# Attention of a gated cross-attention and MoE layer: probabilities transposed in 32x32 blocks on VectorE, V multiplied in eight PE tiles of 32 rows, both layernorms applied by ScalarE

## The chip, the cores and the metric

The kernel runs on one core of one Trainium2 chip. The metric is device time in microseconds (us), the median of the runs of one kernel. Everything is fp32.

## The reference, cut to what matters

Two residual steps on x (4 x 1024 x 256). The first is cross-attention with 16 heads of 64 on a context of 64 rows per batch, with the queries multiplied onto the result; the second is a mixture of 8 experts, two per token.

```python
n = _layernorm(x)
qh = einsum('bld,hdk->hblk', n, w_qs)          # kh, vh: the same from the context, 64 rows per batch
attn = softmax(einsum('hblk,hbmk->hblm', qh, kh))
out = einsum('hblm,hbmk->hblk', attn, vh) * qh
x = x + tanh(g_xattn) * (out.reshape(heads together) @ w_proj.T + b_proj)
n = _layernorm(x)
x = x + tanh(g_ffn) * sum over the 2 chosen experts e of weight_e * (silu(n @ w1[e]) @ w2[e])
```

## The kernel before, in words

**Tiling.** The 4096 tokens are cut into 8 groups of 512 (`NG`), two per batch (`GB`), and each group into 4 tiles of 128 tokens (`T`). The 16 heads are handled as 8 pairs (`NP`), since two heads of 64 fill 128 partitions. Queries are held transposed: `qT` is two blocks (`halves`, L359), each of 4 pairs x 512 tokens, with the 2 x 64 head columns on the partitions.

**Attention of a group.** `queries` (L366) makes one pair's `qT` in one PSUM bank and ScalarE copies it out. `probabilities` (L381) takes one tile of 128 tokens: 8 matmuls of 128 columns give the scores `sc` of all 16 heads, VectorE takes the maximum and subtracts it, ScalarE takes Exp, VectorE sums and inverts, GpSimd multiplies (L404). The result `pr` has the tokens on the partitions. `transpose_probabilities` (L408) turns it round on TensorE: 8 transposes of 128x128 into two PSUM banks, and two copies by ScalarE into `aT` (L415), one per bank. `attend` (L419) takes two pairs of two heads: 4 matmuls, each of 64 rows (the keys of one head) by 64 columns (its V) over all 512 tokens, in four different quarters of the PE array, into two banks `po`; VectorE then multiplies each bank onto the queries in place (L437). `project` (L439) multiplies with `wp` and adds into x.

**Layernorm.** `ln_stats` (L250) makes mean and variance on VectorE, the root on ScalarE and the reciprocal on VectorE. `ln_norm` (L266) has VectorE make `xn` (subtract the mean, multiply by 1/std, L277), TensorE transposes it and ScalarE copies it to `nT`. It runs once per group ahead of the attention ("a") and once after it ("b"); there `keep_b` also goes to DRAM for the experts' gathers.

**V.** `values` (L333) makes V of two batches in four PSUM fills, and ScalarE copies each in four pieces into one SBUF block `vs`, with the keys of even heads on the lower 64 partitions and those of odd heads on the upper 64.

**Order of the work.** The main loop (L1109 to L1164) goes through the groups g and, inside, the tiles t. In step (g, t) it writes down, in this order, the probabilities of tile t, the transposes of the tile before, pieces of the coming queries (`parts`, L1099), at t = 1 the four `attend` calls of group g-1 with queries between them, at t = 2 and 3 the projection of group g-1, the second layernorm of group g-2, the routing, and from g = 6 on pieces of the experts' work (`pieces`). The framework plans each engine's order from this text order and from when operands and buffers are due by its own plan, so neighbouring steps can be interleaved; `keep_in_program_order` and `issue_after` pin single instructions. After the attention the rest of the experts' slots (28 in all) run one after the other.

**Buffers.** PSUM has 8 banks: `ps1` has four single ones, which `pq`, `pa`, `po`, `pp`, `pt` and others share, and `ps2` has two of two banks, which the scores use. SBUF blocks of 8 KB per partition come in three shares (L93): "group" (8), "hidden" (2) and "weight" (7). "weight" holds `wq`, `wp`, two blocks of keys and `vs`, and from g = 6 on the experts' weights as blocks come free. Those weights, the lists of tokens and all first loads are issued on SP's queue, in order.

Of the kernel before, what the change touches and what calls it, by code (L numbers as in the profile page):

```python
# [8 lines left out]
F32 = mybir.dt.float32  # L9
# [12 lines left out]
def kernel(  # L22
# [15 lines left out]
):  # L38

# [83 lines left out]
    normed = dram.tile([N, D], F32, tag="normed", name="normed")  # L123
    lists = dram.tile([E * N + BEHIND, 2], I32, tag="lists", name="lists")
# [66 lines left out]
    vs = block([P, B, NP, DK], "vs", "weight")  # L191
# [58 lines left out]
    def ln_stats(groups, name):  # L250
        n = len(groups) * T
        mv = small.tile([P, n, 2], F32, tag="mv", name=f"mv_{name}")
        for i in range(n):
            st = small.tile([P, 6], F32, tag="st", name=f"st_{name}_{i}")
            first = nc.vector.bn_stats(st, xg[groups[i // T]][:, i % T, :])
            if i == 0 and name[0] == "a":
                tc.keep_in_program_order(first)
            nc.vector.bn_aggr(mv[:, i, :], st)
        rstd = small.tile([P, n, 1], F32, tag="rstd", name=f"rstd_{name}")
        root = nc.scalar.activation(rstd, mv[:, :, 1:2], AF.Sqrt, bias=eps)  # L260
        if name in ("a0", "a1"):
            tc.keep_in_program_order(root)
        nc.vector.reciprocal(rstd, rstd)
        return {g: (mv[:, k * T : (k + 1) * T], rstd[:, k * T : (k + 1) * T]) for k, g in enumerate(groups)}

    def ln_norm(g, stats, name):  # L266
# [8 lines left out]
        for t in range(T):  # L275
            xn = keep[:, t, :] if keep else work.tile([P, D], F32, tag="xn", name=f"xn_{name}_{g}_{t}")
            nc.vector.tensor_scalar(  # L277
                xn, xg[g][:, t, :], mv[:, t, 0:1], rstd[:, t, :], ALU.subtract, ALU.mult
            )
            for c in range(NC):  # L280
                nc.tensor.transpose(  # L281
                    pt[c][:, t * P : (t + 1) * P], xn[:, c * P : (c + 1) * P], ident
                )
# [49 lines left out]
    def values(ctxT):  # L333

        n = 512 // P
        for b0 in range(0, B, 2):
            for p0 in range(0, NP, n):
# [9 lines left out]
                pvv = pv.rearrange("p (q j r k) -> p q j r k", j=2, r=2, k=DK)  # L347
                q0 = p0 // 2
                for i in range(2):
                    to = vs[:, b0 + i].rearrange("p (q r) k -> p q r k", r=2)  # L350
                    for j in range(2):
                        nc.scalar.copy(
                            to[j * M : (j + 1) * M, q0 : q0 + n // 2],
                            pvv[i * M : (i + 1) * M, :, j],
                        )
                yield


    def halves(name, share="group"):  # L359

        return [block([P, NP // 2, G], f"{name}_{i}", share) for i in range(2)]

# [18 lines left out]
    def probabilities(g, t, qT):  # L381

        sc = ps2.tile([P, NP // 2, 2, 2, M], F32, tag="ps2", name=f"sc_{g}_{t}")
        for p in range(NP):
            nc.tensor.matmul(  # L385
                sc[:, p // 2, :, p % 2, :],
# [5 lines left out]
        scv = sc.rearrange("p q r j m -> p (q r j) m")  # L392
# [15 lines left out]
    def transpose_probabilities(g, t, pr, aT):  # L408
        prv = pr.rearrange("p (i j) m -> p i (j m)", j=2)
        n = 512 // P  # L410
        for p0 in range(0, NP, n):
            pt = bank(f"pa_{g}_{t}_{p0}")
            for i in range(n):
                nc.tensor.transpose(pt[:, i * P : (i + 1) * P], prv[:, p0 + i, :], ident)  # L414
            nc.scalar.copy(  # L415
                aT[p0 // n][:, :, t * P : (t + 1) * P], pt.rearrange("p (i q) -> p i q", i=n)
            )

    def attend(g, q, qT, aT):  # L419

        po = [bank(f"po_{g}_{2 * q + j}") for j in range(2)]
        for r in range(2):
            for j in range(2):
                half = slice(j * M, (j + 1) * M)
                i = q * 2 + r
                nc.tensor.matmul(  # L428
                    po[j][r * DK : (r + 1) * DK],
                    vs[half, g // GB, i, :],  # L430
                    of_pair(aT, i)[half],
                    start=True,
                    stop=True,
                )
        for j in range(2):
            own = of_pair(qT, 2 * q + j)
            nc.vector.tensor_tensor(own, po[j], own, ALU.mult)  # L437
# [671 lines left out]
    for g in range(NG + 3):  # L1109
        attention_ends = g >= NG  # L1110
        if g < NG:
            qT, aT = qTs[g], halves(f"aT_{g}", "hidden" if g % 2 and g + 1 < NG else "group")
            held[g] = (qT, aT)
# [5 lines left out]
        for t in range(T):  # L1119
            if g < NG:  # L1120
                pr = probabilities(g, t, qT)
# [5 lines left out]
            if 0 < g <= NG and t == 1:  # L1127
                for q in range(NP // 2):
                    attend(g - 1, q, *held[g - 1])
                    for h, p in products[q : q + 1]:  # L1130
                        queries(h, qTs[h], [p])
                products = products[NP // 2 :]
# [5 lines left out]
            if g == 0:  # L1138
                for _ in range(value_parts[t]):
                    next(pending_values)  # L1140
            if 0 <= before_last < NG and t < 2:
# [73 lines left out]
```

## Time and profile before

| | |
|---|---|
| time, median of 3 runs | 889.93 us (888.75 to 890.03) |
| the profiled execution's own time | 918.12 us |
| its span, first to last instruction | 916.3 us |
| mean granted TensorE clock in it | 0.986 |
| busy: PE, PEld, DVE, ACT, POOL | 871.4, 657.5, 327.8, 263.9, 403.0 us |

PE is TensorE's matmuls, PEld its weight loads, which lie beside matmuls; DVE is VectorE, ACT ScalarE, POOL GpSimd, SP the queue of most DMAs. A line of a group reads: line, engine, operation, output <- inputs, shapes, count | busy us, mean ns of one | idle time of the engine ahead of it, and what ended it. Busy time is the union of the records, and a matmul's record is longer than the time until the next can start, so "mean ns" of matmuls is a latency and not a rate. Each fp32 matmul of the program appears as two passes, each with a weight load of its own: `pq` is 128 matmuls in the program and x256 in the trace. Transposes appear once.

The profiled execution is 28 us longer than the median of the runs. It holds two odd stretches: ScalarE idles from 403.8 to 421.2 us and TensorE waits for it, and from 490 to 512 us TensorE is busy for 12.8 us of 22 only, at a granted clock of 0.88 and 0.53.

### The profile page before, as it was taken

Reading aid. Unit: us, or ns where it says so; the run is one execution under the profiler, and the core shown is the slowest. Engines: PE = TensorE matmul, PEld = TensorE weight load, DVE = VectorE, ACT = ScalarE, POOL = GpSimd, SP = SyncE. Lnnn points to the kernel's source line nnn. Section 1 sums busy time; section 2 is a strip of 40 time slices with the busy share of each in tenths; the row PEclk is TensorE's granted clock in tenths of the full one; section 3 lists DMA queues with packets and bytes.
Section 4 is the critical chain, followed back from the end, with each engine's and each line's share of the span. In section 5 each row is a group of like instructions: output and inputs, shape, how many; then the busy total and the mean of one; then the engine's idle time right before and its main releaser. Section 6 shows DMA issues by size and latency. Waiting matters only on the chain.

```text
span 916.3 us, 11723 instructions
## 1 busy us (share of the span) xinstructions
PE 871.4 (95%) x4328; PEld 657.5 (72%) x4328; DVE 327.8 (36%) x729; ACT 263.9 (29%) x414; POOL 403.0 (44%) x392
## 2 busy tenths in 40 slices
PE   8999999999999998997997899999999999999995
PEld 5556858574857576865885787777777777888884
DVE  3467585777468748631155300000000001100010
ACT  4653353425242425432140121211211211121110
POOL 2051212146213553065447565555455555564443
PEclk9999999999999999998998899999999999999998
DMA  9600000001010225276372575744444564457111
GB/s 203 195 1 1 24 24 24 24 19 30 1 46 1 47 90 188 72 141 143 115 262 63 143 248 166 237 149 140 148 140 142 176 198 148 135 188 267 51 36 42
DMA packets 85279, 102.33 MB, mean 112 GB/s; under 512 B 29366, under 2 KB 71740, under 8 KB 85216
## 3 DMA queue, kind: packets, MB, share of 16 engines
q1 hardware_dynamic: 62656, 66.96, 24.4%
q0 software_dynamic: 11600, 25.25, 8.8%
q10 hardware_dynamic: 10960, 9.31, 3.7%
q8 instruction: 36, 0.59, 0.3%
q14 instruction: 27, 0.22, 0.1%
HBM read 84.75 MB, written 17.33 MB: 111 GB/s over the span
## 4 chain that ended last, share of the span: by engine, by line
PE 80%; DVE 10%; another core or an unknown queue 3%; issue 3%; DMA 1%; POOL 1%; ACT 1%; POOLq 0%; ACTq 0%; DVEq 0%
PE py L978 23%; PE ph L899 22%; PE pp L445 11%; PE pq L370 10%; PE sc L385 5%; PE pa L414 2%; PE pt L867 2%; PE po L428 2%; DVE qT L437 1%; PE pk L317 1%; DVE sm L401 1%; DVE pr L396 1%; DVE mx L394 1%; PE pt_b L281 1%
## 5 line engine op out<-in xcount | busy, mean ns | idle before, releaser
L978 PE MATMUL py<-w,hT 128*128 128x256 f32 (+1 forms) x1168 | 238.3, 369 | 9.2 <-issue 8.7
L899 PE MATMUL ph<-xT,w 128*128 128x256 f32 (+2 forms) x896 | 233.8, 418 | 2.1 <-ACT xT L872 1.2
L978 PEld LDWEIGHTS py<-w,hT 128*128 128x128 f32 (+1 forms) x1168 | 199.8, 184 | 40.2 <-issue 14.0
L899 PEld LDWEIGHTS ph<-xT,w 128*128 128x128 f32 x896 | 170.0, 191 | 57.5 <-issue 1.6
L907 ACT ACTIVATE hT<-ph 128x1024 f32<-128x1024 f32 (+3 forms) x84 | 69.9, 835 | 370.6 <-PE ph L899 319.5
L966 DVE TENSOR_SCALAR x<-py,ids 128x256 f32<-128x256 f32 (+1 forms) x72 | 33.5, 465 | 381.9 <-PE py L978 348.3
L404 POOL TENSOR_TENSOR pr<-pr,sm 128x1024 f32<-128x1024 f32 x32 | 60.9, 1902 | 218.1 <-DVE sm L402 202.1
L370 PE MATMUL pq<-nT_a,wq 128*128 128x512 f32 x256 | 117.0, 597 | 0.4 <-issue 0.2
L445 PE MATMUL pp<-wp,qT 128*128 128x256 f32 x512 | 113.2, 379 | 0.0
L445 PEld LDWEIGHTS pp<-wp,qT 128*128 128x128 f32 x512 | 97.0, 190 | 18.2 <-issue 5.3
L922 POOL DMA_INDIRECT x<-out_dram,ids x68 | 69.3, 1018 | 81.7 <-DMA out_dram<-x,ids 61.9
L845 POOL DMA_INDIRECT x<-normed,ids x68 | 67.9, 999 | 53.4 <-DMA ids<-lists 34.3
L970 POOL TENSOR_TENSOR x<-x,x 128x256 f32<-128x256 f32 (+1 forms) x67 | 48.3, 721 | 90.5 <-DVE x L966 77.8
L370 PEld LDWEIGHTS pq<-nT_a,wq 128*128 128x128 f32 x256 | 45.9, 190 | 53.5 <-issue 47.6
L939 POOL DMA_INDIRECT out_dram<-x,ids x68 | 69.0, 1015 | 23.2 <-POOL x L970 18.0
L568 POOL DMA_INDIRECT lists<-entry,to_row x64 | 62.1, 971 | 20.5 <-issue 17.9
L385 PEld LDWEIGHTS sc<-keys,qT 128*128 128x128 f32 x512 | 62.9, 192 | 7.9 <-issue 7.5
L385 PE MATMUL sc<-keys,qT 128*128 128x128 f32 x512 | 67.4, 278 | 0.0
L415 ACT COPY aT<-pa 128x512 f32<-128x512 f32 x64 | 34.6, 590 | 91.2 <-PE pa L414 71.1
L394 DVE TENSOR_REDUCE mx<-sc 128x16 f32<-128x1024 f32 x32 | 39.0, 1220 | 29.5 <-PE sc L385 28.3
L401 DVE TENSOR_REDUCE sm<-pr 128x16 f32<-128x1024 f32 x32 | 38.9, 1215 | 20.9 <-ACT pr L399 20.9
L377 ACT COPY qT<-pq 128x512 f32<-128x512 f32 x64 | 35.7, 582 | 28.4 <-PE pq L370 28.4
(209 smaller groups left out, 624.8 us busy)
## 6 DMA issues: line engine op xcount, KB each, us to landing
w<-in_L_ffn_w_dram SPq DMA_DIRECT2D x56, 1024.0 KB
out_dram<-x ACTq DMA_DIRECT2D x8, 512.0 KB
normed<-keep_b ACTq DMA_DIRECT2D x8, 512.0 KB
x<-in_x_dram SPq DMA_DIRECT2D x7, 512.0 KB
x<-normed,ids POOLq DMA_INDIRECT x68
x<-out_dram,ids POOLq DMA_INDIRECT x68
out_dram<-x,ids POOLq DMA_INDIRECT x68
wq<-in_L_xattn_w_qs_dram SPq DMA_DIRECT2D x4, 256.0 KB
```

Source lines behind the costliest of these rows:

```text
L370: nc.tensor.matmul(pq, wq[:, c, p * P : (p + 1) * P], nT[g][:, c, :], start=(c == 0), stop=(c == NC - 1),)
L385: nc.tensor.matmul(sc[:, p // 2, :, p % 2, :], of_pair(qT, p)[:, t * P : (t + 1) * P], kT[g // GB][:, p, :], start=True, stop=True,)
L404: nc.gpsimd.tensor_tensor(pr, pr, sm.unsqueeze(2).to_broadcast([P, H, M]), ALU.mult).ins
L445: nc.tensor.matmul(pp[:, i, :], of_pair(qT, p)[:, t * P : (t + 1) * P], wp[:, p, :], start=(p == 0), stop=(p == NP - 1),)
L568: nc.gpsimd.indirect_dma_start(out=lists, out_offset=bass.IndirectOffsetOnAxis(ap=to_row[:, k, i : i + 1], axis=0), in_=entry[:, k, i, :], ...
L845: gather = nc.gpsimd.indirect_dma_start(out=xin[t][:n], out_offset=None, in_=normed[: tokens_of(s)], in_offset=bass.IndirectOffsetOnAxis(a ...
L899: nc.tensor.matmul(ph[:, i, :], a[:, c, f * P : (f + 1) * P], xT[:, c, :], start=(c == 0), stop=(c == NC - 1),)
L907: nc.scalar.activation(hT[f0 // per_tile][:, f1 : f1 + step, :], ph, AF.Silu)
L922: gather = nc.gpsimd.indirect_dma_start(out=acc[t][:r], out_offset=None, in_=outf[:n], in_offset=bass.IndirectOffsetOnAxis(ap=ids[:r, t, 0 ...
L939: put = nc.gpsimd.indirect_dma_start(out=outf[:n], out_offset=bass.IndirectOffsetOnAxis(ap=ids[:r, t, 0:1], axis=0), in_=acc[t][:r], in_of ...
L970: nc.gpsimd.tensor_tensor(acc[t][:r], acc[t][:r], y[t][:r], ALU.add)
L978: nc.tensor.matmul(py[t][rows], hT[f // per_tile][:, f % per_tile, t * P : t * P + r], b[:, f, columns], start=(f == 0), stop=(f == NF - 1),)
```

## The change: what it does

1. **Transposes.** The TensorE transposes `pa` and ScalarE's copies of them are gone. `transpose_probabilities` is two `nc.vector.transpose` of 128x512 per tile, SBUF to SBUF. They transpose each 32x32 block where it stands: the tokens of quarter a of the partitions stay in quarter a, and the 32 partitions of a quarter now hold 32 keys.
2. **V.** As every quarter of the partitions now needs the same keys' V for its own tokens, V must lie in all four quarters. `values` writes it whole to an SBUF block (one copy of 128x512 per bank), stores it to DRAM (`v_dram`, two DMAs of 512 KB), and `load_values` brings each batch back with 8 DMAs of 128 KB, 32 partitions each, into a block `v_b` of the share "weight". Batches 0 and 1 are loaded at (0, 3), batch 2 at (3, 0), batch 3 at (5, 0), all on SP's queue.
3. **attend.** It takes a half of the heads (8) at once, with 64 matmuls of 32 rows by 64 columns over 128 tokens, in four row quarters and two column halves of the array, into four banks `po`, one per row quarter; two matmuls (two sets of 32 keys) accumulate in each place. VectorE multiplies four banks onto the queries, as before 128x512 each, now with the tokens in runs of 32. The two calls of group g-1 stand at the head of steps (g, 1) and (g, 2), ahead of the probabilities.
4. **Scores** are laid out head by head instead of pairs interleaved.
5. **Layernorm.** `ln_stats` makes -mean/std with one more VectorE instruction, and `xn` is made by ScalarE as Identity with scale and bias per partition.

```diff
+    v_dram = dram.tile([B * M, H * DK], F32, tag="v", name="v_dram")
-    vs = block([P, B, NP, DK], "vs", "weight")
+    U = P // T
...
+        nc.vector.scalar_tensor_tensor(mv[:, :, 0:1], mv[:, :, 0:1], -1.0, rstd, ALU.mult, ALU.mult)
...
-            nc.vector.tensor_scalar(
-                xn, xg[g][:, t, :], mv[:, t, 0:1], rstd[:, t, :], ALU.subtract, ALU.mult
-            )
+            nc.scalar.activation(xn, xg[g][:, t, :], AF.Identity, bias=mv[:, t, 0:1], scale=rstd[:, t, :])
...
+                nc.scalar.copy(made[:, b0 // 2, p0 * P : (p0 + n) * P], pv)
                 yield
+            nc.sync.dma_start(v_dram[b0 * M : (b0 + 2) * M, :], made[:, b0 // 2])
+
+    def load_values(b):
+        v_of[b] = block([P, M // U, H, DK], f"v_{b}", "weight")
+        for m in range(M // U):
+            rows = v_dram[b * M + m * U : b * M + (m + 1) * U, :].rearrange("m (h k) -> m h k", k=DK)
+            for a in range(T):
+                nc.sync.dma_start(v_of[b][a * U : (a + 1) * U, m], rows)
...
-        for p0 in range(0, NP, n):
-            pt = bank(f"pa_{g}_{t}_{p0}")
-            for i in range(n):
-                nc.tensor.transpose(pt[:, i * P : (i + 1) * P], prv[:, p0 + i, :], ident)
-            nc.scalar.copy(
-                aT[p0 // n][:, :, t * P : (t + 1) * P], pt.rearrange("p (i q) -> p i q", i=n)
+        n = H * M // 2
+        for h in range(2):
+            nc.vector.transpose(
+                aT[h][:, t], pr.rearrange("p h m -> p (h m)")[:, h * n : (h + 1) * n].rearrange("p (b u) -> p b u", u=U)
             )
...
+    def attend(g, h, qT, aT):
+        po = [bank(f"po_{g}_{h}_{a}") for a in range(T)]
+        for i in range(NP // 2):
+            for m in range(M // U):
+                for r in range(2):
+                    for a in range(T):
+                        quarter = slice(a * U, (a + 1) * U)
+                        nc.tensor.matmul(
+                            po[a][r * DK : (r + 1) * DK, i * T * U : (i + 1) * T * U],
+                            v_of[g // GB][quarter, m, h * NP + 2 * i + r, :],
+                            aT[h][quarter, :, (2 * i + r) * (M // U) + m, :],
+                            start=(m == 0),
+                            stop=(m == M // U - 1),
+                        )
+        own = qT[h].rearrange("p i (t a u) -> p a i t u", t=T, u=U)
+        for a in range(T):
+            nc.vector.tensor_tensor(
+                own[:, a], po[a].rearrange("p (i t u) -> p i t u", t=T, u=U), own[:, a], ALU.mult
+            )
...
+            if 0 < g <= NG and t in (1, 2):
+                attend(g - 1, t - 1, *held[g - 1])
             if g < NG:
                 pr = probabilities(g, t, qT)
...
-            if 0 < g <= NG and t == 1:
-                for q in range(NP // 2):
-                    attend(g - 1, q, *held[g - 1])
-                    for h, p in products[q : q + 1]:
-                        queries(h, qTs[h], [p])
-                products = products[NP // 2 :]
...
+            if (g, t) == (0, T - 1):
+                load_values(0)
+                load_values(1)
+            elif g % GB == GB - 1 and g > GB - 1 and g // GB + 1 < B and t == 0:
+                load_values(g // GB + 1)
```

More of the change, by code (lines that the diff above doesn't have):

```diff
@@ L190 @@
     kT = [keys_of[b // 2][:, b % 2] for b in range(B)]
-    vs = block([P, B, NP, DK], "vs", "weight")
+    U = P // T
+    assert T == 4 and M % U == 0
+    v_of = {}
     ident = const.tile([P, P], F32, tag="ident", name="ident")
@@ L335, in values @@
         n = 512 // P
+        made = block([P, B // 2, H * DK], "values", "weight")
         for b0 in range(0, B, 2):
@@ L346, in values, with for_probabilities @@
                     )
[L347 to L351, printed above, removed]
-                        nc.scalar.copy(
-                            to[j * M : (j + 1) * M, q0 : q0 + n // 2],
-                            pvv[i * M : (i + 1) * M, :, j],
-                        )
-                yield
+                nc.scalar.copy(made[:, b0 // 2, p0 * P : (p0 + n) * P], pv)
+                yield
+            nc.sync.dma_start(v_dram[b0 * M : (b0 + 2) * M, :], made[:, b0 // 2])
[5 more added lines that the diff above has]
+                nc.sync.dma_start(v_of[b][a * U : (a + 1) * U, m], rows)
     def halves(name, share="group"):
         return [block([P, NP // 2, G], f"{name}_{i}", share) for i in range(2)]
+    def for_probabilities(name, share):
+        return [block([P, T, NP * M // U, U], f"{name}_{i}", share) for i in range(2)]
     def of_pair(t, p):
@@ L381, in probabilities @@
     def probabilities(g, t, qT):
-        sc = ps2.tile([P, NP // 2, 2, 2, M], F32, tag="ps2", name=f"sc_{g}_{t}")
+        sc = ps2.tile([P, NP, 2 * M], F32, tag="ps2", name=f"sc_{g}_{t}")
         for p in range(NP):
             nc.tensor.matmul(
-                sc[:, p // 2, :, p % 2, :],
+                sc[:, p],
                 of_pair(qT, p)[:, t * P : (t + 1) * P],
@@ L391, in probabilities @@
             )
-        scv = sc.rearrange("p q r j m -> p (q r j) m")
+        scv = sc.rearrange("p q (r m) -> p (q r) m", m=M)
         mx = small.tile([P, H], F32, tag="mx", name=f"mx_{g}_{t}")
@@ L408, in transpose_probabilities @@
     def transpose_probabilities(g, t, pr, aT):
-        prv = pr.rearrange("p (i j) m -> p i (j m)", j=2)
-        n = 512 // P
-        for p0 in range(0, NP, n):
-            pt = bank(f"pa_{g}_{t}_{p0}")
-            for i in range(n):
-                nc.tensor.transpose(pt[:, i * P : (i + 1) * P], prv[:, p0 + i, :], ident)
-            nc.scalar.copy(
-                aT[p0 // n][:, :, t * P : (t + 1) * P], pt.rearrange("p (i q) -> p i q", i=n)
-            )
[L419 to L437, printed above, removed]
+        n = H * M // 2
+        for h in range(2):
+            nc.vector.transpose(
+                aT[h][:, t], pr.rearrange("p h m -> p (h m)")[:, h * n : (h + 1) * n].rearrange("p (b u) -> p b u", u=U)
+            )
+    def attend(g, h, qT, aT):
[17 more added lines that the diff above has]
+            )
     def project(g, qT, t0):
@@ L1111 @@
         if g < NG:
-            qT, aT = qTs[g], halves(f"aT_{g}", "hidden" if g % 2 and g + 1 < NG else "group")
+            qT, aT = qTs[g], for_probabilities(f"aT_{g}", "hidden" if g % 2 and g + 1 < NG else "group")
             held[g] = (qT, aT)
@@ L1140 @@
                     next(pending_values)
+                if t == T - 1:
+                    for _ in pending_values:
+                        pass
+            if (g, t) == (0, T - 1):
[3 more added lines that the diff above has]
+                load_values(g // GB + 1)
             if 0 <= before_last < NG and t < 2:
```

## The prediction, made before the changed kernel ran

> **What bounds the kernel now.** First the windows of the attention (40 to 412 us, 46 us per group), two of eight here: length, then busy us of PE, PEld, DVE, ACT, POOL, granted clock, DMA share, GB/s.
>
> ```profile
> 135.00:180.00 45.00, 44.73 (x256) 31.60 (x255) 25.83 (x44) 17.06 (x26) 9.97 (x5) 1.00 0.07 24
> 180.00:225.00 45.00, 42.54 (x219) 28.96 (x217) 37.39 (x84) 19.20 (x29) 22.76 (x18) 1.00 0.12 24
> ```
>
> PE is full: over the eight windows it is busy for 358 of 372 us, DVE for 245, ACT for 155. Only where routing falls (second line) does DVE come near. What leaves PE here shortens the kernel; the other engines matter when they hold up PE. After 512 us PE is full again with the experts, so a gain is carried to the end.
>
> Then the groups of the tiles concerned, each shape apart (line, engine, operation, tiles, shape, count | busy us, mean ns | idle before):
>
> ```profile
> L428 PE MATMUL po<-aT,vs 64*64 64x512 f32 x256 | 37.2, 609 | 3.8 <-DVE qT L437 2.7 <-issue 0.9
> L437 DVE TENSOR_TENSOR qT<-po,qT 128x512 f32<-128x512 f32 x64 | 40.3, 676 | 6.5 <-PE po L428 5.5 <-remote 1.0
> L415 ACT COPY aT<-pa 128x512 f32<-128x512 f32 x64 | 34.6, 590 | 91.2 <-PE pa L414 71.1 <-remote 9.0 <-DVE mv_b L258 7.9
> L414 PE MATMUL pa<-ident,pr 128*128 128x128 f32 x256 | 33.5, 274 | 1.1 <-POOL pr L404 1.1
> L277 DVE TENSOR_SCALAR keep_b<-x,mv_b,rstd_b 128x256 f32<-128x256 f32 x32 | 15.5, 529 | 0.2
> L277 DVE TENSOR_SCALAR xn_a<-x,mv_a,rstd_a 128x256 f32<-128x256 f32 x28 | 13.2, 504 | 2.5 <-PE pt_a L281 2.5
> L491 DVE TENSOR_TENSOR cmp<-lg 128x512 f32<-128x512 f32 x4 | 2.7, 683 | 0.0
> ```
>
> A matmul's record is a latency; its price comes from the timeline (start, busy us) and the chain of work:
>
> ```profile
> 144.96 1.04 PE L414 MATMUL pa<-ident,pr 128*128 128x128 f32 x8
> 126.43 1.95 PE L428 MATMUL po<-aT,vs 64*64 64x512 f32 x16
> 120.29 0.21 PEld L428 LDWEIGHTS po<-aT,vs 64*64 64x64 f32 x8 [0.17 <-issue]
> ```
> ```profile
> 88.89 6.91 PE pp L445 x32
> ```
>
> 32 passes of 256 columns in 6.91 us are 0.216 us each: 0.84 ns per column. Eight transposes in 1.04 us, with the last one's 0.27 us latency taken off, are 0.77/7 = 0.110 us each. Sixteen `po` passes of 512 columns would take 16 x 0.43 = 6.9 us in turn; they took 1.95, so four quarters of the array work at once. Eight weight loads of 131 ns each fit into 0.21 us; single records start 6 to 7 ns apart.
>
> **What the Trainium skill says.** "TensorEngine Tiling (Array Packing)", Tiling Modes: 32x64 gives eight tiles that load weights and multiply in parallel, and a change of the mode drains the array. The trace agrees for 64x64 (above) and shows the drain: between `pq` and `po` 0.09 us more than the stream, and as much back; between `sc` and `pa` none. Eight tiles it doesn't show. "TensorE: Matmul & The Clock Gate", "Wait — 56ns, not 53.3ns?": starts of matmuls never come closer than about 25 ns, and 62 ns where microcode decodes them. The trace differs for short bursts in different tiles (6.6 ns); its longest such burst is 16 instructions (`pl`, 8 passes). At 367.93 us PE's sequencer ends a semaphore wait and 12 instructions of `pl` have started 0.224 us later: at most 19 ns each, so microcode at 62 ns per matmul is out. "VectorE: DVE Perf Modes", The three transpose paths: 32x32 blocks only, 311 ns for 128x128 in bf16; no row here shows it. "ScalarE: Activation LUTs", Table sets: Identity lies in every set, so it costs no table load; ScalarE's copies here cause none between Exp and Sqrt.
>
> **The change part by part.**
>
> *Transposes off PE.* 256 x 0.110 = 28.2 us leave PE, all on the path. ScalarE loses 64 copies, 34.6 us, off the path.
>
> *V in eight tiles.* Before: 256 passes of 512 columns, four at once: 64 x 0.43 = 27.5 us. After: 1024 matmuls, 2048 passes of 128 columns. Eight at once: 256 x 0.108 = 27.6 us, plus about 0.09 per call for the first weights, 16 x 0.09 = 1.4: 29 us, so +1.5. This asks for 16 instructions (8 loads, 8 passes) per 0.108 us, 6.8 ns each, through 256 instructions per call. The pairs seen start every 6.6 ns, so it is just possible. Bounds: not below 27.6, as the same columns stream; above, 19 ns per instruction, less the 64 or so queued: 192 x 19 = 3.6 us per call against 1.75, +30 us; with four tiles at once 55 us, +28. I take +1.5. Changes of mode: 19 stretches of `po` become 16, 6 x 0.09 = -0.6.
>
> *Banks.* A call needs all four banks of `ps1`. What PE wrote last there, a `pq`, is copied out by ScalarE in 0.58 us; with signalling PE waits 0.7, 16 x 0.7 = +11.2, unless scores are put there first. After the call VectorE frees a bank every 0.68 us, 2.7 for four; the scores that follow (16 passes of 0.11, other banks) cover 1.8, and the next `pq` needs one bank: nothing, but 0.9 per call (14 us) if VectorE comes late. The waits of `po` and `pt_b` for VectorE's evictions today go: 2.7 + 0.9 + 2.2 = -5.8 (PE's waits in this stretch). Range -6 to +20; I take +5.4.
>
> *VectorE.* 60 `xn` and `keep_b` go (28.7 us; with the first four, 30.1), 13 small products of 0.2 come (2.6), and 64 transposes of 512 columns. Nearest row: 128x512 at 0.683. The page's 311 ns and the slope of this trace's rows (1221 - 683 over 512) give 311 + 384 x 1.05 = 714 ns as an estimate; I take 0.7: 45 us. Lower bound 0.41 (a 128x256 operation), upper 1.2, if four-byte elements go at half speed: 26 to 77 us. VectorE goes to 245 - 30 + 3 + 45 = 263 of some 350 us; at the upper bound 295. Hidden by PE; where routing falls, 37.4 becomes 39 of 42, nearly no cover. In VectorE's queue the transposes wait for GpSimd's product, one tile (12 us) behind; behind them stand the next tile's maximum and the evictions.
>
> *ScalarE.* 64 `xn` come: by the page's price for two pointer operands (What ACT_TABLE_LOAD costs) 186 + 2 x 93 + 0.833 x 256 = 585 ns, an estimate; at most 37 us. They replace 34.6 of copies and some 3.5 on V: about even. Behind them in its queue stand copies of `pq`; ScalarE is at 42%, so nothing.
>
> *V by way of DRAM.* Two stores and 32 loads, 5 MB. The last `pv` pass starts at 55.3 us, the first `po` at 77.6 (some 74 after). Store, 16 issues of 0.38 us on SP and landing end near 66 to 70: hidden by 4 us or more; bare, one wait of that size. Batches 2 and 3 come while SP issues nothing and DMA is at 0.07. At (6, 0) one block of "weight" less is free for the experts until (6, 2): one 1 MB load later, with its use a step away: nothing.
>
> Sum: -28.2 + 1.5 - 0.6 + 5.4 = **-21.9 us**. The profiled execution, 918.1, would become 896.2. It stands 28 us above the median because of two stretches with idle engines (404 to 421 and 490 to 512 us), neither caused by a part of the change; I take the difference to the median: 889.9 - 21.9 = **868.0**.
>
> **Rivals.**
> 1. *Slower: PE doesn't keep eight tiles busy.* Instructions come too slowly for passes of 0.108 us, or two passes of one tile block what is behind them. For it: no burst over 16 instructions is on record, and a call has 256. Against: `po` passes of one tile are overtaken by other tiles. Price at four at once: +27.6, so 889.9 + 5.7 = **895.6**; at two, 110 us and 951. It decides from 21.9/256 + 0.113 = 0.20 us per round of eight.
> 2. *VectorE and banks take the gain.* Transposes at 1.2 us, banks at +20: -28.2 + 1.5 - 0.6 + 20 = -7, **882.6**. For it: the routing windows. Against: VectorE still has 15% left.
> 3. *The gain is lost later:* the experts' part waits for lists or weights anyway, half remains, **879**. Against: from 512 us on PE is full.
>
> **How the numbers follow.** Forecast, 854 to 876: 0.50. Rivals 2 and 3, 876 to 888: 0.12. Rival 1: 0.33, of which 0.2 up to 906. Below 854: 0.05. Within 0.2% of 889.9, about what a measurement can tell from no change, 0.05 of these in all. Faster 0.62, same 0.05, slower 0.33. Range 854 to 906.
>
> **What would show it.** Eight transposes per tile gone; `po` calls of 128 passes in about 1.8 us; VectorE's transposes near 0.7 us; PE's idle time ahead of `po` near 0.7 us per call. The prediction is wrong if a `po` call takes over 3 us, or if PE's idle time in the attention grows by more than 20 us.

## The result, and the profile after

The changed kernel takes 936.13 us (median of 4 runs, 932.54 to 939.34) against 889.64 us before (888.75 to 890.03): ratio 1.0523, 95% interval 1.0474 to 1.0572. The prediction, 868.0 us with a range of 854 to 906, was wrong in sign. The profiled execution of the changed kernel took 938.70 us, its span is 937.0 us, and the granted clock fell from 0.986 to 0.961. The profiled execution before was a slow one, but its two odd stretches begin at 403 us, and what is compared of it below by groups lies ahead of them.

The same two windows of the attention as before (length, then busy us of PE, PEld, DVE, ACT, POOL, granted clock, DMA share, GB/s):

```profile
135.00:180.00 45.00, 37.70 (x400) 27.40 (x400) 24.62 (x42) 12.73 (x21) 9.95 (x5) 0.92 0.15 45
180.00:225.00 45.00, 38.85 (x306) 28.86 (x305) 33.29 (x63) 11.79 (x19) 14.30 (x10) 0.89 0.08 15
```

TensorE was busy for 44.73 and 42.54 us of 45 at clock 1.00; now it is busy for 37.70 and 38.85 at 0.92 and 0.89. No other engine has filled up: VectorE does less than before in both windows. Work was taken off TensorE, and TensorE lost more to idle time than it was spared.

The groups that answer to those shown of before (line numbers have moved):

```profile
L435 PE MATMUL po<-aT,v 32*64 32x128 f32 x2048 | 47.9, 290 | 11.9 <-ACT qT L388 7.5
L422 DVE STREAM_TRANSPOSE aT<-pr 128x512 f32<-128x512 f32 x64 | 42.4, 691 | 37.2 <-POOL pr L414 37.0
L444 DVE TENSOR_TENSOR qT<-po,qT 128x512 f32<-128x512 f32 x64 | 39.5, 678 | 14.7 <-PE po L435 14.7
L284 ACT ACTIVATE keep_b<-x,mv_b,rstd_b 128x256 f32<-128x256 f32 x32 | 17.1, 594 | 4.3 <-DVE mv_b L270 4.3
```

VectorE's transposes cost what was forecast (691 ns against 0.7 us), and so does ScalarE's layernorm (594 ns against 585). The `pa` groups are gone. What stands out is the last column of `aT`: VectorE stood for 37 us with a transpose at the head of its queue, waiting for GpSimd's product. The list of TensorE's waits between 40 and 480 us (waiter, releaser: us in total, times, longest) names who paid:

```profile
PE pq L381 <- DVE qT L444: 34.6, 6, 6.7
PE po L435 <- ACT qT L388: 7.5, 6, 2.5
PE pp L454 <- DVE qT L444: 4.9, 1, 4.9
```

`qT L444` is the multiplication that empties the four banks of `po`. In seven groups TensorE waited for it 3.3 to 6.7 us each, 39.5 us in all. Before, all its waits for that multiplication were 4.9 us:

```profile
PE po L428 <- DVE qT L437: 2.7, 3, 1.5
PE pt_b L281 <- DVE qT L437: 2.2, 7, 0.6
```

One of the long ones in the timeline (start, us, engine, line, operation; in brackets the idle time ahead and its releaser), first TensorE:

```profile
136.57 2.67 PE L435 MATMUL po<-aT,v 32*64 32x128 f32 x128
139.17 1.60 PE L395 MATMUL sc<-keys,qT 128*128 128x128 f32 x12
146.69 3.78 PE L381 MATMUL pq<-nT_a,wq 128*128 128x512 f32 x4 [5.91 <-DVE qT L444]
150.26 1.98 PE L454 MATMUL pp<-wp,qT 128*128 128x256 f32 x7
```

then VectorE in the same time:

```profile
137.85 1.30 DVE L422 STREAM_TRANSPOSE aT<-pr 128x512 f32<-128x512 f32 x2 [0.71 <-POOL pr L414]
139.08 1.18 DVE L411 TENSOR_REDUCE sm<-pr 128x16 f32<-128x1024 f32 x1
140.18 1.21 DVE L404 TENSOR_REDUCE mx<-sc 128x16 f32<-128x1024 f32 x1
141.31 0.24 DVE L412 RECIPROCAL sm<-sm 128x16 f32<-128x16 f32 x1
141.47 1.18 DVE L406 TENSOR_TENSOR pr<-sc,mx 128x1024 f32<-128x1024 f32 x1
143.63 1.30 DVE L422 STREAM_TRANSPOSE aT<-pr 128x512 f32<-128x512 f32 x2 [0.98 <-POOL pr L414]
144.86 1.18 DVE L411 TENSOR_REDUCE sm<-pr 128x16 f32<-128x1024 f32 x1
145.95 2.47 DVE L444 TENSOR_TENSOR qT<-po,qT 128x512 f32<-128x512 f32 x4
```

The call ends at 139.2. VectorE is idle for only 0.98 us of this time: it works through the softmax of two tiles and a pair of transposes, and only at 145.95, 6.7 us late, takes the four multiplications. All four banks of `ps1` are `po`'s until then, so `pq` can't start. The first `pq` passes show a second price: 4 passes take 3.78 us, about half the usual rate. The Trainium skill, "TensorE: Matmul & The Clock Gate", The HAM clock gate, says that an idle TensorE falls to half clock after some 3.4 us. The trace agrees: TensorE is idle from 140.8 us, and from 144.0 to 150.8 the granted clock is 0.50:

```profile
144.00:150.80 6.80, 4.12 (x6) 1.96 (x7) 4.72 (x9) 0.30 (x1) 1.90 (x1) 0.50 0.21 51
```

The trace records 11 stretches of 3.4 to 10.2 us at clock 0.5 in the attention of the changed kernel, and 3 in the whole kernel before, the first at 419 us. From the first `po` of the first group to the first of the last one, the passes of `pq` and `pp`, their waits taken off, take 187.7 us against 172.9 before: 15 us more, nearly all of it inside these stretches.

### The profile page after: what moved, and what is told of

It reads as the page before. It is cut to its first block, busy times and chain, and to the rows that moved or that the text cites. A ratio compares the mean times of both kernels' runs of the same rounds, so it can differ in the third digit from the quotient of the medians.

```text
span 937.0 us, 14810 instructions
## 1 busy us (share of the span) xinstructions
PE 864.8 (92%) x5864; PEld 667.6 (71%) x5864; DVE 344.1 (37%) x742; ACT 253.9 (27%) x398; POOL 404.0 (43%) x392
## 4 chain that ended last, share of the span: by engine, by line
PE 69%; DVE 15%; ACT 5%; POOL 4%; DMA 3%; issue 3%; SPq 0%; POOLq 0%; ACTq 0%
PE py L987 23%; PE ph L908 22%; PE pp L454 12%; PE pq L381 5%; DVE mx L404 3%; POOL pr L414 2%; DVE sm L411 2%; DVE aT L422 2%; DVE qT L444 2%; DVE pr L406 2%; PE po L435 2%; ACT pr L409 2%; PE pt L876 2%; PE sc L395 1%; ACT L409 1%
## 5 line engine op out<-in xcount | busy, mean ns | idle before, releaser
L987 PE MATMUL py<-w,hT 128*128 128x256 f32 (+1 forms) x1168 | 232.6, 366 | 0.0
L381 PE MATMUL pq<-nT_a,wq 128*128 128x512 f32 x256 | 126.5, 639 | 34.6 <-DVE qT L444 34.6
L454 PE MATMUL pp<-wp,qT 128*128 128x256 f32 x512 | 119.3, 393 | 4.9 <-DVE qT L444 4.9
L454 PEld LDWEIGHTS pp<-wp,qT 128*128 128x128 f32 x512 | 102.1, 200 | 27.9 <-issue 7.3
L381 PEld LDWEIGHTS pq<-nT_a,wq 128*128 128x128 f32 x256 | 49.1, 203 | 84.8 <-issue 47.1
L435 PE MATMUL po<-aT,v 32*64 32x128 f32 x2048 | 47.9, 290 | 11.9 <-ACT qT L388 7.5
L422 DVE STREAM_TRANSPOSE aT<-pr 128x512 f32<-128x512 f32 x64 | 42.4, 691 | 37.2 <-POOL pr L414 37.0
L435 PEld LDWEIGHTS po<-aT,v 32*64 32x64 f32 x2048 | 39.2, 136 | 22.9 <-ACT qT L388 11.5
```

The lines of the kernel that those rows point to most:

```text
L381: nc.tensor.matmul(pq, wq[:, c, p * P : (p + 1) * P], nT[g][:, c, :], start=(c == 0), stop=(c == NC - 1),)
L435: nc.tensor.matmul(po[a][r * DK : (r + 1) * DK, i * T * U : (i + 1) * T * U], v_of[g // GB][quarter, m, h * NP + 2 * i + r, :], aT[h][quar ...
L454: nc.tensor.matmul(pp[:, i, :], of_pair(qT, p)[:, t * P : (t + 1) * P], wp[:, p, :], start=(p == 0), stop=(p == NP - 1),)
L987: nc.tensor.matmul(py[t][rows], hT[f // per_tile][:, f % per_tile, t * P : t * P + r], b[:, f, columns], start=(f == 0), stop=(f == NF - 1),)
```

## The experiments

Runs with the same time before in the table share a chip, and ratios are to the kernel before on that chip. On some chips it takes 916 to 926 us instead of 889; why isn't known (in e3's profile, taken on one of them, TensorE has 6 us of gaps that have no releaser). So times are compared between runs of one chip only. "us a group" is from the first `po` of the first group to that of the last, divided by seven, in the profiled execution.

| run | before | time | ratio (95%) | us a group |
|---|---|---|---|---|
| before | 889.64 | | | 46.9 |
| changed | 889.64 | 936.13 | 1.052 (1.047 to 1.057) | 53.6 |
| e1 evict first | 916.6 | 947.2 | 1.042 (1.012 to 1.072) | 51.6 |
| e2 changed, norm on VectorE | 916.6 | 972.0 | 1.067 (1.036 to 1.097) | 55.6 |
| e3 before, norm on ScalarE | 916.6 | 917.7 | 1.005 (1.001 to 1.009) | 46.7 |
| e4 evict first, norm on VectorE | 916.6 | 966.7 | 1.062 (1.045 to 1.079) | 54.1 |
| e5 changed again | 916.5 | 967.7 | 1.055 (1.051 to 1.060) | 55.0 |
| e6 evict first again | 916.5 | 948.1 | 1.027 (1.019 to 1.035) | 51.1 |
| e7 query copies first | 916.5 | 971.3 | 1.063 (1.056 to 1.069) | 55.4 |
| e8 scores first | 916.5 | 946.3 | 1.031 (1.027 to 1.034) | 51.3 |
| e9 before + idle transposes | 889.3 | 910.0 | 1.024 (1.022 to 1.026) | 48.5 |
| e10 wide products | 889.3 | 917.7 | 1.033 (1.031 to 1.035) | 47.5 |
| e11 products twice | 889.3 | 972.3 | 1.092 (1.090 to 1.095) | 56.8 |
| e12 scores between | 889.3 | 918.3 | 1.032 (1.030 to 1.034) | 50.6 |
| e13 evict first, control | 921.3 | 954.6 | 1.031 (1.023 to 1.039) | 51.5 |
| e14 e8, product on VectorE | 921.3 | 948.8 | 1.028 (1.020 to 1.036) | 52.1 |
| e15 e12, product on VectorE | 921.3 | 960.8 | 1.033 (1.021 to 1.044) | 53.4 |
| e16 changed, product on VectorE | 921.3 | 972.5 | 1.055 (1.048 to 1.062) | 55.7 |
| e17 e12, order at second call | 925.7 | 957.6 | 1.031 (1.025 to 1.038) | 52.6 |
| e18 before without transposes | 925.7 | 910.4 | 0.983 (0.979 to 0.986) | 44.3 |

**The order on VectorE: e1 with e2 to e4.** The softmax of a step and its transposes are queued behind the call's last multiplication; e3 and e2 do and undo the layernorm part alone.

```diff
-                attend(g - 1, t - 1, *held[g - 1])
-            if g < NG:
-                pr = probabilities(g, t, qT)
-            if last:
-                transpose_probabilities(*last)
+                behind = tc.issue_after(attend(g - 1, t - 1, *held[g - 1]))
+            with behind:
+                if g < NG:
+                    pr = probabilities(g, t, qT)
+                if last:
+                    transpose_probabilities(*last)
```

> The changed kernel with one more order on VectorE: in the two steps with a call of attend, the softmax and the transposes of that step are queued behind the call's last multiplication by the queries. Theory A (the loss is the place of those multiplications in VectorE's queue: TensorE waits some 6 us per group for a bank of po, and then runs at a lower granted clock): the waits of pq and pp for qT, 39 us in all, shrink to under 8, the granted clock in the attention goes from 0.93 back to 0.98 or more, and the time to 875 to 890 us. Rival B (VectorE has too much work since it transposes): its queue only trades places, the waits move to the next tile's scores and transposes, and the time stays within 925 to 945. Rival C (eight tiles of TensorE are slow by themselves): the waits go, but calls of 2.3 to 2.6 us and the banks ahead of a call keep the time over 905.

> The changed kernel with the third part undone: VectorE subtracts the mean and scales again, 64 operations of 0.4 to 0.5 us, 30 us more work on it; ScalarE loses 33. Theory A: this doesn't touch the order that costs; within 10 us of the changed kernel's 936. Rival B (VectorE overloaded): 945 or more. Rival D (ScalarE, which now makes the normed rows, copies queries out late and holds up the calls): 920 or less.

> The kernel before with the third part alone: ScalarE makes the normed rows with scale and bias, VectorE one small product per statistic. Theory A: 885 to 895, as VectorE and ScalarE both have room and TensorE's work is the same. Rival D: over 905, since ScalarE also copies the transposes and the queries out.

> The order of e1 and the norms on VectorE together. Theory A: within 8 us of e1, and 875 to 895. Rival B: 15 us or more above e1. Rival D: 10 us or more below e1.

TensorE's waits for the multiplications fell to 9.6 us in e1 (6.4 of `pq`, 3.2 of `pt_b`). Its time fell far less than expected (1.042, not 875 to 890 us), and the times scatter too widely to price it, so e5 and e6 repeat the changed kernel and e1 side by side. The layernorm on ScalarE alone costs nearly nothing (e3: 0.5%, at most 0.9%). With VectorE as loaded as in the changed kernel it pays: e4, which gives the layernorm back to VectorE, is 20 us above e1, and all its four runs (962.6 to 969.9) lie above all of e1's (939.2 to 959.3). That is what rival B, too much work on VectorE, had asked for (15 us or more). e2 has no partner on its chip; it is 4 us above e5, the changed kernel on another chip of that kind.

**The same, beside each other: e5 to e8.** e7 adds to e1 that ScalarE's layernorms stand behind the copies of the queries. e8 writes the call after the scores, the maximum and Exp of the tile, so that only the sum and the transposes stand behind the multiplications.

```diff
-            nc.scalar.copy(of_pair(qT, p), pq)
+            copied[:] = [nc.scalar.copy(of_pair(qT, p), pq).ins]
...
+            with tc.issue_after(copied[0]) if g < NG else nullcontext():
                 if 0 <= before_last < NG and t < 2:
                     norm_again(before_last, t)
```

> The changed kernel as it is, beside the next three on one chip, since e1 to e4 ran on a chip where the kernel before itself took 917 us. Every theory: 1.04 to 1.06 of the kernel before.

> The kernel of e1 again, beside the changed one on one chip. Theory A: at least 20 us below the changed kernel. In e1's trace groups without a starved TensorE took 44 to 46 us against 54 in the changed kernel and 48 in the kernel before, so on a chip where TensorE isn't starved of instructions the time is 885 or less. Rival B: the same as the changed kernel.

> The kernel of e1 with one more order, on ScalarE: the normed rows and what belongs to the norms are queued behind the copies of the queries of the same step. Theory D' (the waits ahead of a call, 6 to 12 us in all, come from copies of queries that stand behind the normed rows on ScalarE): those waits go below 4 us and the time is 3 to 10 us below e6. Otherwise within 3 us of e6.

> The changed kernel with the call of attend written down after the scores, the maximum, the subtraction and Exp of its step, and VectorE's sum and transposes queued behind the call's multiplications. TensorE then has the scores to do while the last queries are copied out, and VectorE has done with the scores when the call ends. Theory A: as e6 or up to 15 us below, as both waits are covered. Rival B: the same as the changed kernel.

The waits for the multiplications, first in e5, then in e6:

```profile
PE pq L381 <- DVE qT L444: 21.6, 4, 6.1
PE pp L454 <- DVE qT L444: 4.9, 1, 4.9
```
```profile
PE pq L381 <- DVE qT L444: 7.4, 3, 6.5
```

The order alone gives back 967.7 - 948.1 = 19.6 us, and these waits fell by 19.1. It doesn't give back what was lost: e6 is still at 1.027. e7 made it worse (`prow` now waited 12.2 us for `chosen`), so this order on ScalarE is no remedy. e8 ended where e6 did, but by another way: its waits for the multiplications stayed at 22.4 us, though none was longer than 4.7.

```profile
PE pq L381 <- DVE qT L451: 20.3, 6, 4.7
PE pp L462 <- DVE qT L451: 2.1, 1, 2.1
```

What it saved lies ahead of the calls and in them. The waits of `po` for copies of the queries fell from 7.5 us in e5 to 1.0, and calls that found all banks free took 1.83 us from first to last pass, the forecast's 1.8 (more on them at e10). All of TensorE's waits from 40 to 480 us are 53 us in e5 and 44 in e6 and in e8. So VectorE's order explains e6's gain, but it is not the only way to win 20 us, and no run has both remedies whole.

**What VectorE's load costs by itself: e9.** The kernel before with transposes that nobody reads.

```diff
+        for n in range(0, H * M, D):
+            nc.vector.transpose(unread, flat[:, n : n + D].rearrange("p (b u) -> p b u", u=32))
```

> The kernel before, unchanged on TensorE, with VectorE's 32x32 transposes of every tile of probabilities added where the changed kernel has them; nobody reads what they write. They are four of 256 columns a tile instead of two of 512 (they go to a buffer that is free), about 1.6 us a tile, 52 us in all. Theory A (what is lost is that VectorE's transposes, waiting for GpSimd, stand ahead of the multiplications that free the banks): TensorE waits for VectorE's multiplications here too, and the time grows by 15 to 45 us. Rival I (the calls of 256 instructions lose it on TensorE itself): TensorE is untouched here, within 0.5% of before.

```profile
L423 DVE STREAM_TRANSPOSE unread<-pr 128x256 f32<-128x256 f32 x128 | 56.0, 438 | 31.4 <-POOL pr L404 30.1
```

TensorE's work is untouched, and the kernel is 20.7 us slower. 56 us of transposes and 31 us of waiting at the head of VectorE's queue are not hidden by TensorE. Rival I had asked for no change. But theory A's picture isn't seen either: unlike in the changed kernel, no wait grew to 6 us, and those for the multiplications are 5.2 us against 4.9 before. From the first `po` of the first group to the first of the last one e9 takes 11 us more, of which 4.8 lie in the passes of `po` and 4.0 in waits, in small pieces. The load is somewhat more than the changed kernel's, since the layernorm stays on VectorE.

**What a call costs on TensorE: e10 to e12.** All are e1 with other calls. e10 uses each block of V for four heads' columns (the wrong V for three in four): 64 instructions a call instead of 256, same tiles, same columns. e11 issues each product twice. e12 puts the next tile's scores between the eighths of a call, four passes after each 32.

```diff
-        for i in range(NP // 2):
+        w = 4
+        for i in range(0, NP // 2, w):
...
+                        first = (2 * i + r) * (M // U) + m
...
-                            po[a][r * DK : (r + 1) * DK, i * T * U : (i + 1) * T * U],
+                            po[a][r * DK : (r + 1) * DK, i * T * U : (i + w) * T * U],
...
-                            aT[h][quarter, :, (2 * i + r) * (M // U) + m, :],
+                            aT[h][quarter, :, first : first + 4 * (w - 1) + 1 : 4, :],
```
```diff
-        for i in range(NP // 2):
+        for i in [k for k in range(NP // 2) for again in range(2)]:
```
```diff
         for i in range(NP // 2):
+            if between and i:
+                between(i)
...
+                    def between(i):
+                        scores(g, t, qT, range(2 * i - 2, 2 * i))
```

> The kernel with the evictions first (the first experiment), but each block of V of 32x64 multiplies 512 columns, those of four heads, instead of 128, those of one: a quarter of the instructions (64 a call instead of 256), the same tiles, the same columns in all. V is that of the wrong head for three heads in four. Rival I (the supply of instructions limits a call[...]): calls of 1.8 to 2.0 us, none over 3 us but for a wait, and 25 to 50 us less than the kernel with the evictions first. Theory S (eight tiles don't stream at once, at most about six): calls stay at 2.3 to 2.5 us, and those of 6 to 12 us stay too if they are no matter of instructions.

> The kernel with the evictions first, each product issued twice into the same place: 512 instructions a call instead of 256. If eight tiles cost 1.75 us a call this adds 28 us, at six of eight 37 us. If instructions come from memory at a lower rate than a call uses them (rival I), it adds far more: the second half of a call goes at the rate of the supply, 60 us or more in all.

> The kernel with the evictions first, with the next tile's scores (16 passes) put between the eighths of a call, two after each 32 instructions. The same work, 14 changes of mode more a call (0.09 us each, 13 to 20 us in all if none is hidden). If a call outruns its instructions only by its density (rival I), the long calls of 6 to 12 us get shorter and the time stays or falls by up to 20 us; if not, it grows by 13 to 20 us.

TensorE's timeline, e10 and then e12 (x32 is a burst of 32 passes, 64 instructions):

```profile
170.69 2.31 PE L437 MATMUL po<-aT,v 32*64 32x512 f32 x32
172.93 1.16 PE L395 MATMUL sc<-keys,qT 128*128 128x128 f32 x8
```
```profile
166.06 0.69 PE L444 MATMUL po<-aT,v 32*64 32x128 f32 x32
166.69 0.71 PE L394 MATMUL sc<-keys,qT 128*128 128x128 f32 x4
167.33 0.69 PE L444 MATMUL po<-aT,v 32*64 32x128 f32 x32
```

In such a burst of e12 the records start in eights: eight passes 6 to 7 ns apart, the second eight 160 ns after the first, and each further one 109 ns on. Eight tiles do stream together, at the full rate. They can do so through a whole call: in e8 two calls of 128 passes, which began behind scores with all banks free, took 1.83 us from first to last pass, two eights per 218 to 234 ns after the first two. One of them, and the scores behind it:

```profile
123.04 2.10 PE L442 MATMUL po<-aT,v 32*64 32x128 f32 x128
125.07 1.16 PE L395 MATMUL sc<-keys,qT 128*128 128x128 f32 x8
```

Those 256 instructions came in 1.83 us, 7.1 ns each, so it is not their number that makes a call of the changed kernel take 2.3 to 2.6 us. Its later passes aren't slow either: in the call at 298.28 us the last 64 passes take 0.92 us, near the full rate, and the first 64 take 1.37. The loss is at the head. In e6's call at 170.8 us three banks are free and the fourth still holds `pl_t`, which VectorE copies out until 0.30 us after the call's start. Six passes run, the first 16 take 0.53 us, and each further 16 take 0.22 to 0.26. A call that begins behind a `pq` waits for its copy by ScalarE in the same way (in the changed kernel at 122.3 us until 0.69 us after the start). So in these calls the traces point to the banks and not to the instructions. e10 fits: with a quarter of the instructions its calls take 2.24 us to the next tile, not the 1.8 to 2.0 expected of rival I and little less than the 2.33 of e6's call above.

e10's lists of tokens differ: its experts have 64 more passes of 256 columns (0.216 us each, 13.8 us), so with the same lists it would be near 904 us, some 14 below e12, an estimate. In its seven groups `po` takes as long as in e12 (40.1 us against 40.9), so the gain isn't in the calls; its waits are 22.4 us against 31.9.

With twice the passes instructions do run short. A call of e11 shows gaps that have no releaser,

```profile
174.09 4.00 PE L435 MATMUL po<-aT,v 32*64 32x128 f32 x248 [0.30 <-ACT qT L388]
180.01 1.94 PE L395 MATMUL sc<-keys,qT 128*128 128x128 f32 x16 [1.92 <-issue]
```

28.1 us of them in `po` altogether, where the changed kernel's profile lists none. Most calls run near 13.7 ns a pass until such a gap of 0.6 to 4.3 us comes, in most of them after 145 to 246 passes. 27.4 us more of columns cost 53.9 us against e12, the nearest run on that chip, which has the scores between besides (e1 itself wasn't repeated there).

e12 takes 918.3 us, a ratio of 1.032 where e1 and e6 were at 1.042 and 1.027 on other chips. Its bursts buy nothing that can be seen, since a change of tile size isn't cheap: 32 passes take 0.63 us to the next scores against 0.43 of streaming, and 4 scores 0.64 against 0.43, about 0.2 us a change, all told, where the prediction used 0.09. The largest waits left in it are elsewhere:

```profile
PE prow L551 <- DVE chosen L518: 11.7, 3, 4.2
PE sc L394 <- DVE rstd_b L268: 7.4, 1, 7.4
```

`chosen` (routing) and `rstd_b` (second layernorm) stand behind the softmax in VectorE's queue, so giving the multiplications precedence made other consumers late. The changed kernel's list has neither wait.

On the chips with the slower kernel before, calls of 256 instructions show such gaps too, and far longer ones. A call of e13 (the control below) there:

```profile
208.50 1.47 PE L435 MATMUL po<-aT,v 32*64 32x128 f32 x47 [2.23 <-ACT qT L388]
210.26 0.48 PE L435 MATMUL po<-aT,v 32*64 32x128 f32 x3 [0.29 <-issue]
211.03 0.58 PE L435 MATMUL po<-aT,v 32*64 32x128 f32 x3 [0.28 <-issue]
213.25 0.71 PE L435 MATMUL po<-aT,v 32*64 32x128 f32 x4 [0.74 <-issue]
```

After 47 passes, three to five come every 0.7 to 1.5 us for six microseconds (a part of the lines is shown). In the runs with such calls on these chips, four to eight of 16 take over 6 us from first to last pass, up to 21.9 (e17); in part this is waiting that has a releaser. What causes the rest isn't settled.

**Is it GpSimd, at the head of VectorE's queue? e13 to e16.** The product with the reciprocal of the sum moves to VectorE in three kernels.

```diff
-        newest[:] = [
-            nc.gpsimd.tensor_tensor(pr, pr, sm.unsqueeze(2).to_broadcast([P, H, M]), ALU.mult).ins
-        ]
+        nc.vector.tensor_tensor(pr, pr, sm.unsqueeze(2).to_broadcast([P, H, M]), ALU.mult)
```

> The kernel with the evictions first once more, as the control of the next three. On the chips where it ran it was at 1.03 to 1.04 of before, with calls of 2.1 to 2.5 us and some of 6 to 12. Expected here 1.03.

> The kernel with a tile's scores, maximum and Exp ahead of the call, and the product with the reciprocal of the sum on VectorE instead of GpSimd (32 times 1.2 us, 38 us more for VectorE). Theory G (what holds VectorE, and with it the banks, is that a transpose at the head of its queue waits for GpSimd): VectorE's 39 us of waiting for GpSimd go, nothing else is late, and the time falls by 10 to 30 us. Rival V (VectorE has no room for 38 us more): no gain, or slower by up to 10 us.

> The kernel with the scores between the eighths of a call (its transposes wait 27 us for GpSimd, once 7.8 us while GpSimd issues gathers, and TensorE then 7.4 us for the statistics behind them), with the product on VectorE. Theory G: the waits of sc for rstd_b and of prow for chosen (19 us together) shrink to less than half, and the time falls by 10 to 25 us, to about before's. Rival V: the waits stay, as VectorE is busy 38 us longer.

> The changed kernel with one edit: the product with the reciprocal of the sum on VectorE instead of GpSimd. Theory G: the wait of pq and pp for VectorE's multiplications (39.5 us in the changed kernel) falls to under 15 us and the time by 15 to 30 us. Theory A in its first form (the order alone: maximum, subtraction, sum and transposes stand ahead of the multiplications, whoever they wait for): the wait stays at 30 us or more, since VectorE gets more work ahead of them.

In e16 the waits for the multiplications are

```profile
PE pq L381 <- DVE qT L442: 19.9, 5, 4.3
PE pp L452 <- DVE qT L442: 6.2, 1, 6.2
```

26.1 us, against 26.5 in e5, and the ratio is e5's. The theory that GpSimd holds VectorE falls: 37 us of waiting became 45 us of work in the same place of the queue. The wait was shorter than the 30 us that the plain order would have had in the expectation, so that number was off as well. e14 and e15 stay where their partners are (1.028 and 1.033, the control 1.031), where that theory had asked for 10 to 30 us less.

**Which call, and was the first step right? e17 and e18.** e17 is e12 with the order kept at a group's second call alone. e18 is the kernel before with the transposes and their copies left out; V multiplies the queries instead of the probabilities.

```diff
-                behind = tc.issue_after(attend(g - 1, t - 1, *held[g - 1], between))
+                multiplied = attend(g - 1, t - 1, *held[g - 1], between)
+                if t == 2:
+                    behind = tc.issue_after(multiplied)
```
```diff
-                transpose_probabilities(*last)
+                pass
...
-                    of_pair(aT, i)[half],
+                    of_pair(qT, i)[half],
```

> The kernel with the scores between the eighths of a call, with VectorE's softmax work and transposes queued behind the multiplications at a group's second call alone; at the first they stand as in the changed kernel. In the changed kernel six of seven waits of pq for the multiplications come after the second call. If the order matters there alone, pq's wait stays under 10 us, the waits behind the softmax (prow for chosen 11.7 us, sc for rstd_b 7.4) shrink, and the time falls by 5 to 15 us. If it matters at both calls, a wait of 3 to 6 us a group returns after the first and the time grows by 10 to 25 us.

> The kernel before with the transposes of the probabilities and ScalarE's copies of them left out; V multiplies the queries instead, so the output and the experts' lists are others, and the attention alone is to be read (start of the first po to start of the last, and the time of a group). If the prediction's first step is right (28.2 us leave TensorE, all on the path), a group takes 3.5 us less than before's 47.7 and the seven groups 25 us less. If something else sets the pace of a group (the chain of softmax on VectorE, ScalarE and GpSimd), under 12 us less.

In e17 `pq` waits for the multiplications for 1.5 us: for this wait the order matters at the second call alone. The time didn't fall further (1.031, e12 1.032): `prow` still waits 10.3 us for `chosen`, and `sc` for `rstd_b` 3.0.

e18 falls by 15.3 us although its experts, with other lists, have 64 passes more (13.8 us): 29 us at equal lists, an estimate. In the attention itself 2.6 us a group are gained, 18 us over seven, between the 25 of the prediction's step and the 12 of its rival. The 24.4 us of `pa` are gone there, but the passes of `po` and `pq` take 3.6 and 1.7 us more, and waits 0.9.

## Why the prediction was wrong, step by step

**Transposes off PE (-28.2): right.** e18 gives 18 us for the attention and, by the estimate, some 29 for the whole kernel. In seven groups of the changed kernel 24.4 us of `pa` are gone, 28 for eight.

**V in eight tiles (+1.5): right for TensorE itself.** Eight tiles stream at once, and a call with free banks takes the 1.8 us of the forecast (e8). In seven groups `po` takes 10.8 us more than before, of which 1.3 were forecast. The traces put most of the other 9.5 down to the banks: the head of a call runs while its last bank is still being copied out. Rival 1, the rate of instructions, did not decide on the chips at 889 us, where e10's quarter of the instructions shortens the calls little. On the chips at 916 to 926 us it may: five of e6's calls take 49 us from first to last pass, where 1.83 each would be 9.

**Banks (+5.4): this is the step that failed.** Its first term fits, in part by luck: 11.2 us of waits for the copies of `pq` ahead of the calls were forecast, 0.7 in each, and `po` idles for 11.9 us, but only 7.5 of them for these copies, in six waits. Its second, "nothing, but 0.9 per call (14 us) if VectorE comes late", measured 39.5 us. The prediction priced the multiplications from the end of the call (four times 0.68 us), as if VectorE took them at once. It had written down what stands ahead of them ("behind them stand the next tile's maximum and the evictions") and charged nothing. The calls now end earlier than VectorE's queue does, and one call holds all four banks, where before a call took two and `pq` ran between. The half clock after such idle time, some 15 us, was in no term. Together: 39.5 + 15 + 9.5 + 0.7 = 65 of the 68 us between forecast and result. This is a tally of the trace and not of experiments. What undoing shows is 19.6 us with the order (e5 and e6), of the 51 that the changed kernel loses on that chip; the waits that the new order brings elsewhere are part of the difference.

**VectorE ("hidden by PE"): wrong, though its busy time was right.** e9 adds such transposes to the kernel before and loses 20.7 us, and e4 shows 20 us for the layernorm's work. In the two windows above VectorE was busy there for 31.50 and 40.38 us of 45: what is left of 45 is no reserve when its instructions are links between TensorE's (scores to softmax, `po` to free banks, statistics to the next transposes). Of the 20.7 us, 11 fall into the seven groups (1.6 us each), in no single wait. They are no further term of the sum above, as in the changed kernel VectorE's lateness shows as the waits counted there. With the order mended, 19 us of waits for `chosen` and `rstd_b` remain in e12, of the 29 that it loses. That they are the rest of the loss isn't shown: in e17 they are 13 us and the ratio is the same.

**ScalarE, V by way of DRAM (nothing): right.** e3 is at 1.005, and an `xn` costs 594 to 602 ns against the 585 estimated; the first call starts at 71.6 us against 77.6, so nothing waited for V.

**Rivals.** Rival 2 (VectorE and banks) was the mechanism, priced at 20 us at most and therefore on the wrong side of zero. Rival 3 (lost later) didn't happen: the experts' part is full after the attention. "PE's idle time in the attention grows by more than 20 us" was named as what would refute the forecast, and it did: from 20 us, 6.5 of them in the first odd stretch, to 55 between 40 and 480 us. Calls of over 3 us, the other sign, came too: seven of 16, with waits inside them.

**What stays open.** Why instructions come so slowly in some calls on some chips isn't settled. The Trainium skill, "Runtime: NRT & Kernel Launch", Instruction fetch mechanics, says that instructions come from memory in blocks of 16 KiB, 256 instructions, and that this is mostly hidden. The trace agrees on the size: the queue named "instruction" took 36 packets and 0.59 MB before, 48 packets and 0.79 MB after, 16 KB each. One call of the changed kernel uses as many instructions as a block holds. e11 and e13 have gaps without a releaser; that they are this fetch is only argued. The head of the calls was read from the traces and has no experiment of its own. No version with the full result beat the kernel before; the best are at 1.027 to 1.033. A third buffer for the probabilities, which would let the transposes stand one tile later, wasn't tried, and whether SBUF has room for it isn't shown.

## What to carry to other kernels

Before an operation is moved to an engine with time to spare, write down that engine's queue around each instruction that frees a buffer, and price the eviction from the end of what stands ahead of it, not from the end of the matmuls. A stage that takes all banks of a pool at once makes that price due in full, and each idle time of 6 us on TensorE then cost some 2 us again in half clock here. It makes the head of the stage wait for whatever used the last bank, too. When a stage runs below its rate, look where in it the time goes before blaming the rate: here the second half of a call ran at full rate, and the first half waited for a bank.

## What the hardware showed that was not expected

- Eight tiles of 32x64 stream at once for a whole call: 128 passes of 128 columns (fp32), with their 128 weight loads, in 1.83 us from first to last, 14.4 ns each (e8). With twice the passes a call shows gaps of 0.6 to 4.3 us that have no releaser (e11).
- A change between 128x128 and 32x64 tiles costs about 0.2 us of TensorE all told (e12: 32 passes in 0.63 us against 0.43).
- A 128x512 fp32 transpose in 32x32 blocks on VectorE takes 691 ns, a 128x256 one 438 ns.
- After 5.9 us of idle time four passes of 512 columns take 3.78 us, at half clock.
